# Second norm on ScalarE and turned by TensorE, and fill and drain slots left to the scheduler, in a fused channel-mix and convolution kernel

## The chip, the core and the metric

The kernel runs on one core of a Trainium2 chip. The metric is the device time of one execution in microseconds (us), the median of the runs shown. The engines are TensorE (PE in the profile, with PEld for its weight loads), VectorE (DVE), ScalarE (ACT), GpSimd (POOL) and SyncE (SP), which here only issues DMAs.

## The reference

The input x has 4 images of 128 channels and 128 x 128 positions, in float32. Two layers follow one another. Cut to what matters:

```python
# layer 0, on t = positions x channels (channels are the last axis)
t = ln(gn(x), g0, b0)
y1 = ln(t, g1, b1)
t = t + (sigmoid(y1) * y1) @ W_out.T
y2 = ln(t, g2, b2)                       # the "second norm" of the change
wht = y2 @ W_whiten.T
k = square(relu(wht @ W_key.T))          # 512 hidden channels
t = t + sigmoid(wht @ W_recep.T) * (k @ W_value.T)
x = x + 2 * t                            # two passes, with H and W exchanged, give the same t
# layer 1
out = conv3x3(gn(x)) + bias              # expert 0's weights, 128 -> 128 channels
x = x + out * se[:, :, None, None]       # se: sigmoid of a small MLP on the image's means
```

Here `gn` is a group norm over whole images in groups of four channels, and `ln` a norm over the channels of one position. So the second layer of an image can start only when the first layer of the whole image is done.

## The kernel before

An image is cut into 32 chunks of 512 positions. Two chunks are a pair, called g (0 to 63), with halves h = 0 and 1. A *slot* s is one pass through the list of operations in ORDER; an entry such as `pk01:2` stands for operation pk with half 0 and index 1 on pair g = s - 2. So each slot works on several pairs at once, at different depths, and the list sets the order of instructions on every engine. All slots stand in `tc.manual_schedule()`: there the instructions go to the engines as written. What stands outside it (the set-up, and the convolution of the last image after the slots) is ordered by the scheduler.

For one half the operations are these. `u` (ScalarE) applies the group norm, `Tu` (TensorE, four 128 x 128 transposes) brings positions onto partitions, `bn0` (VectorE) takes the statistics per position, `nb0` (GpSimd, small rows L377 to L388 with a power L382) makes the factors, `t` (ScalarE) scales, and `g` and `b` (GpSimd) apply gain and shift. `bn1`, `nb1`, `z1` (ScalarE), `Tz1`, `silu`, `att`, `T` are the first inner norm and the attention-like part. `tt` turns t back. `bn2` and `nb2` give the factors of the second norm.

The second norm itself: its mean is taken out by weights whose mean over channels is removed at set-up (`mean_of`). Its factor 1/std lies on the partitions, one number a position, but is needed along the free axis. So `Tr` (L429) turns the factors into rt, `rc` (L433) copies it into rrow, `W` (L437) stores it to DRAM, `R` (L442) reads it back spread over all partitions, and `cp` (L446, VectorE) multiplies the turned t by it into y2. Then come `pk` (L450, four matmuls a half into 512 hidden channels), `re` (L454, relu on ScalarE), `sq` (L459, square on ScalarE), `pr` and `th` for the gate, `kv` (L476, four accumulating matmuls), `S` (L486, adds 2t to x), `q` (L492), `x` (L496, GpSimd) and `bx` (L502, statistics for the convolution's group norm).

The convolution of the image before runs in the same slots, from slot 20 on: it is a Winograd form F(4,3) along one axis, with six products c0 to c5 a block of 16 rows (three matmuls each, L514 to L516) and the rest on VectorE. Of its operations half belong to even slots and half to odd ones (EVEN and ODD). The convolution of the last image, 8 blocks, follows after the slots.

PSUM holds eight banks: two each for the tags h (pk, pr), tr (z1t, att, rt, tt) and ut, one for kv and one for conv.

Of the kernel before, what the change touches and what calls it, by code (L numbers as in the profile page):

```python
# [19 lines left out]
LN_EPS = 1e-5  # L20

LAG = 4


ORDER = """
    u1:0 Tu1:0 u0:0 x11:3 Tz10:1 Tu0:0 bn01:0 bn00:0 z11:1 bx1:3 v1:1 pr0:2 Tz11:1 q2:1
    silu0:1 p2:1 re00:2 sq00:2 y2:1 ca:1 att0:1 silu1:1 c0:1 pk01:2 nb0:0 d8:1 kv00:2 T0:1
    y0:1 th0:2 t1:0 bn20:1 v3:1 tt1:2 g1:0 re01:2 in0:0 c1:1 cp1:2 e1:1 att1:1 pk02:2 c3:1
    T1:1 bn21:1 pk10:2 c5:1 b1:0 y3:1 re02:2 S1:2 t0:0 nb2:1 e3:1 pk03:2 v2:1 g0:0 b0:0
    re10:2 c2:1 in1:0 a:1 pk12:2 sq01:2 sq10:2 Tr:1 v0a:1 sq02:2 re03:2 sq03:2 re12:2 b:1  # L30
    kv01:2 kv02:2 rc:1 pk13:2 re13:2 v4:1 pk11:2 kv03:2 sq12:2 c4:0 bn11:0 v5a:0 tt0:1
    bn10:0 v0b:1 pr1:2 q0:2 c:0 d:0 re11:2 sq11:2 S0:1 sq13:2 kv10:2 v5b:0 kv11:2 th1:2
    kv12:2 kv13:2 nb1:0 W:1 y1:0 R0:1 z10:0 q:0 cp0:1 pk00:1 R1:1 x10:2 p:0 bx0:2 q1:2
"""

SQUARES = ("AAAA", "AAAA")

ON_GPSIMD = set()
ODD = {"v5a", "v5b", "c4", "c", "d", "y1", "y2", "ca", "d8", "c0", "y0", "c5", "y3"}
# [7 lines left out]
def conv_preact_kernel(  # L47
# [57 lines left out]
    wk = ctx.enter_context(tc.tile_pool(name="wk", bufs=2))  # L105
    small = ctx.enter_context(tc.tile_pool(name="small", bufs=4))
    stat = ctx.enter_context(tc.tile_pool(name="stat", bufs=2))
    dram = ctx.enter_context(tc.tile_pool(name="dram", bufs=2, space=bass.MemoryType.DRAM))
    ps = ctx.enter_context(tc.tile_pool(name="ps", bufs=2, space=bass.MemoryType.PSUM))

    def bank(tag, name, bufs=2):
        return ps.tile([P, CH], F32, tag=tag, name=name, bufs=bufs)
# [3 lines left out]
    def load_block(g):  # L116
        b, k = g // NBLK, g % NBLK
        blocks[g] = xp.tile([P, BLK], F32, tag="x", name=f"x_{b}_{k}")
        nc.sync.dma_start(
            blocks[g],  # L120
            x[b, :, k * BLK_ROWS : (k + 1) * BLK_ROWS, :].rearrange("c h w -> c (h w)"),
        )
# [20 lines left out]

    nhalf = const.tile([P, N], F32, tag="nhalf", name="nhalf")
    nc.gpsimd.memset(nhalf, -0.5)
    mean_of = const.tile([P, P], F32, tag="mean_of", name="mean_of")
    nc.gpsimd.memset(mean_of, 1.0 / C)

    def load_const(name, src, shape):
        t = const.tile(shape, F32, tag=name, name=name)  # L150
# [22 lines left out]

    wk_s = const.tile([P, HID], F32, tag="wk_s", name="wk_s")
    wr_s = const.tile([P, P], F32, tag="wr_s", name="wr_s")
    kbias = const.tile([P, NH], F32, tag="kbias", name="kbias")
# [2 lines left out]
    def staged(name, n):  # L182
        return wk.tile([P, n], F32, tag="h", name=name, bufs=6)
# [5 lines left out]
    for src, n, dst, bias in ((wkt, HID, wk_s, kbias), (wrt, P, wr_s, rbias)):  # L189
        pw = bank("h", "pw")  # L190
        nc.tensor.matmul(pw[:, :n], ww, src, start=True, stop=True)
        raw, raw2 = staged("raw", n), staged("raw2", HID)
        nc.vector.tensor_copy(raw, pw[:, :n])
        nc.vector.tensor_scalar(raw2[:, :n], raw, g2, None, ALU.mult)
        pc = bank("h", "pc")
        nc.tensor.matmul(pc[:, :n], mean_of, raw2[:, :n], start=True, stop=True)
        nc.vector.tensor_tensor(dst, raw2[:, :n], pc[:, :n], ALU.subtract)
        pb = bank("h", "pb")
        for j in range(n // P):
            nc.tensor.matmul(pb[:, j : j + 1], raw[:, ts(j, P)], b2, start=True, stop=True)  # L200
        nc.vector.tensor_copy(bias, pb[:, : n // P])
# [31 lines left out]
    def input_norm(b):  # L233
        _, mg, rs = yield from group_norm(st0.pop(b), "0")
        nb = col("nb0")
        nc.vector.scalar_tensor_tensor(nb, mg, -1.0, rs, ALU.mult, ALU.mult)
        gn0[b] = rs, nb

    def conv_setup(b):
# [27 lines left out]
        nc.vector.tensor_scalar(dg, ident, se, None, ALU.mult)  # L267
        yield
        pg = bank("h", "pg")
        nc.tensor.matmul(pg[:, :P], mean_of, dg, start=True, stop=True)  # L270
        yield
        row = wk.tile([P, P], F32, tag="u", name="row")
        nc.scalar.mul(row, pg[:, :P], float(C))
        yield
        nc.vector.scalar_tensor_tensor(
            cw, cw, rs, row.rearrange("p (o c) -> p o c", o=1).to_broadcast([P, 9, P]),
# [10 lines left out]
            uw[i] = wg.tile([P, 3, P], F32, tag="uw", name=f"uw{i}", bufs=9)  # L287
            u[i] = uw[i].rearrange("p b c -> p (b c)")

        w6 = wk.tile([P, 3 * P], F32, tag="z", name="w6", bufs=2)  # L290
        nc.scalar.mul(w6, w1, 1.0 / 6)
        tmp = wk.tile([P, 3 * P], F32, tag="u", name="tmp")
        nc.vector.tensor_tensor(tmp, w0, w2, ALU.add)
# [3 lines left out]
        nc.vector.scalar_tensor_tensor(u[1], tmp, -1.0 / 6, w6, ALU.mult, ALU.subtract)  # L297
        nc.vector.scalar_tensor_tensor(u[2], tmp, -1.0 / 6, w6, ALU.mult, ALU.add)
        yield
        w4 = wk.tile([P, 3 * P], F32, tag="z", name="w4", bufs=2)  # L300
        nc.scalar.mul(w4, w0, 0.25)
        nc.scalar.mul(w6, w6, 0.5)
        nc.vector.tensor_tensor(tmp, w4, w2, ALU.add)
# [17 lines left out]
    def flat(t):  # L321
        return t.rearrange("p s c -> p (s c)")
# [23 lines left out]
    def sub_tile(tag, name, bufs):  # L346
        return wk.tile([P, SUB, C], F32, tag=tag, name=name, bufs=bufs)
# [19 lines left out]
    def norm_terms(k, g):  # L367

        st = S.pop(("st", k, g))

        def term(name):
            return small.tile([P, N], F32, tag=f"{name}{k}", name=name, bufs=2)

        gp, rs, nb, sm = nc.gpsimd, term("rs"), term("nb"), term("sm")
        gp.tensor_tensor(rs, st[:, :, 1], st[:, :, 4], ALU.subtract)  # L377
        gp.tensor_tensor(rs, rs, rs, ALU.mult)
        gp.tensor_scalar(rs, rs, C / 4, C * LN_EPS, ALU.mult, ALU.add)
        gp.tensor_tensor(sm, st[:, :, 2], st[:, :, 5], ALU.add)  # L380
        gp.tensor_tensor(rs, rs, sm, ALU.add)
        gp.tensor_tensor(rs, rs, nhalf, ALU.pow)  # L382
        S["norm", k, g] = rs, nb
        if k == 2:
            return
        gp.tensor_tensor(sm, st[:, :, 1], st[:, :, 4], ALU.add)
        gp.tensor_tensor(sm, sm, nhalf, ALU.mult)
        gp.tensor_tensor(nb, sm, rs, ALU.mult)  # L388

    def first_norm(g, h):  # L390
        if ("t", g) not in S:
# [9 lines left out]
        nc.gpsimd.tensor_tensor(t, t, over(b0), ALU.add)  # L401

    def norm(k, g, h):
        S[f"z{k}", g, h] = z = sub_tile("z", "z", 2)
        scaled(z, S["t", g][:, h], S["norm", k, g], h)

    def norm_turned(k, g, h):
# [13 lines left out]
        t = flat(S["t", g][:, h])  # L421
        nc.vector.tensor_tensor(t, S.pop(("att", g, h)), t, ALU.add)

    def turn_std(g):
        rs, _ = S.pop(("norm", 2, g))
        S["rt", g] = rt = bank("tr", "rt")
        nc.tensor.transpose(rt[:N, :P], rs, ident)  # L429

    def copy_std(g):
        S["rrow", g] = row = small.tile([N, P], F32, tag="rrow", name="rrow", bufs=1)
        nc.vector.tensor_copy(row, S.pop(("rt", g))[:N, :P])  # L433

    def store_std(g):
        S["rd", g] = rd = dram.tile([N, P], F32, tag="rd", name="rd")
        nc.sync.dma_start(rd, S.pop(("rrow", g)))  # L437

    def spread_std(g, h):
        S["R", g, h] = r = wk.tile([P, CH], F32, tag="R", name="R", bufs=3)  # L440
        src = S["rd", g][h * SUB : (h + 1) * SUB, :]
        nc.sync.dma_start(r, src.rearrange("(o s) c -> o (s c)", o=1).to_broadcast([P, CH]))  # L442

    def key_input(g, h):
        S["y2", g, h] = y = wk.tile([P, CH], F32, tag="y2", name="y2")
        nc.vector.tensor_tensor(y, flat(S["tt", g, h]), S.pop(("R", g, h)), ALU.mult)  # L446

    def key(g, h, j):
        S["pk", g, h, j] = pk = bank("h", "pk")
# [34 lines left out]
    def add_t(g, h):  # L484
        xs = chunk_of(g, h)
        nc.vector.scalar_tensor_tensor(  # L486
            xs, flat(S["tt", g, h]), 2.0, xs, ALU.mult, ALU.add
        )

    def gated(g, h):  # L490
# [140 lines left out]
    def layer0_op(op, g):  # L631
# [12 lines left out]
            "silu": lambda: silu(g, *d),  # L644
            "att": lambda: attend(g, *d),
            "T": lambda: attended(g, *d),
            "Tr": lambda: turn_std(g),
            "rc": lambda: copy_std(g),
            "W": lambda: store_std(g),
            "R": lambda: spread_std(g, *d),  # L650
            "cp": lambda: key_input(g, *d),
            "pk": lambda: key(g, *d),
            "re": lambda: key_relu(g, *d),
# [32 lines left out]
    for _ in input_norm(0):  # L686
        pass

    with tc.manual_schedule():
        loaded = NBLK  # L690
        for s in range(slots):
            chains = []
            b = s // NP
            if s % NP == NP - 2 and b + 1 < B:
                chains.append(input_norm(b + 1))
            if s % NP == done and 0 < b:
                chains.append(conv_setup(b - 1))
            if s % 2 and s + 1 >= NP and loaded < B * NBLK:
                load_block(loaded)
                loaded += 1  # L700
            for g in reads.get(s, ())[:1]:
                fetch_stats(g)
            for n, (op, k) in enumerate(order):
                g = s - k
                if op in EVEN or op in ODD:
                    c = g - NP - LAG
                    if 0 <= c < (B - 1) * NP and (c % 2 == 1) == (op in ODD):
                        conv_op(op, c // 2)
                elif op in ("in0", "in1"):
                    h = int(op[2])  # L710
                    for i in reads.get(s, ())[:1]:
                        in_stats(i, h, S["in", i][:, ts(h, CH)])
                elif 0 <= g < B * NP:
                    layer0_op(op, g)
                if n % 5 == 4:
                    for chain in chains:
                        next(chain, None)
            for chain in chains:
                for _ in chain:
                    pass  # L720
            for i in reads.get(s, ())[1:]:
                fetch_stats(i)
                for h in range(PAIR):
                    in_stats(i, h, S["in", i][:, ts(h, CH)])


    for k in range((B - 1) * NBLK, B * NBLK):
# [47 lines left out]
```

## Time and profile before

| what | value |
|---|---|
| median of 3 runs (1998.43 to 2006.08) | 2001.2 us |
| the profiled execution, its own time | 2001.2 us |
| its span | 1999.4 us |
| TensorE, VectorE, ScalarE, GpSimd busy | 92%, 67%, 65%, 58% of the span |
| DMA | 130.72 MB, 65 GB/s over the span |

Busy time is a share of the span; a span begins with the first recorded instruction and ends with the last. A row of a group of instructions gives line, engine, operation, tiles, count, busy time, the mean of one in ns, and then the idle time of that engine just before these instructions, with what ended it. TensorE lists one float32 matmul as two instructions, so 128 x 512 matmuls that follow one another take 0.86 us each.

### The profile page before, as it was taken

What the parts mean: (1) busy time and instruction counts of PE and PEld (TensorE: products, weight loads), DVE (VectorE), ACT (ScalarE), POOL (GpSimd) and SP (SyncE); (2) the same over time, 40 slices, a digit from 0 to 9 for tenths busy, and PEclk for the clock granted to TensorE, in tenths of its full rate; (3) what the DMA queues carried; (4) which work ended last, traced back from release to release, by engine and by line L of the source; (5) the groups of instructions that cost most, each with busy time, mean ns of one, the idle gap of its engine ahead of it and who ended that gap; (6) DMA issues with size and microseconds to landing.
All of it is one profiled execution on the core that took longest, in us unless ns stands there. A gap on an engine that the chain in (4) does not pass through costs nothing.

```text
span 1999.4 us, 21672 instructions
## 1 busy us (share of the span) xinstructions
PE 1835.4 (92%) x6154; PEld 937.8 (47%) x6154; DVE 1338.9 (67%) x3276; ACT 1297.7 (65%) x2526; POOL 1151.2 (58%) x1939
## 2 busy tenths in 40 slices
PE   2388888888899999999999999999999999998898
PEld 1244444444455555555455455554454555543343
DVE  5355555555677777687677777766766667664897
ACT  0488787888767676777677777676676777752100
POOL 0577667666666666666566667666566676640000
PEclk9899999999999999999999999999999999998999
DMA  5111111111111222122122222111011111110112
GB/s 196 42 43 43 54 50 57 41 66 65 62 57 61 95 85 85 53 96 76 43 75 85 95 74 86 64 64 55 32 64 64 56 62 64 43 42 33 42 63 84
DMA packets 38567, 130.72 MB, mean 65 GB/s; under 512 B 5408, under 2 KB 7088, under 8 KB 30256
## 3 DMA queue, kind: packets, MB, share of 16 engines
q1 hardware_dynamic: 36160, 128.47, 18.1%
q10 hardware_dynamic: 2288, 0.87, 0.2%
q8 instruction: 49, 0.80, 0.2%
q14 instruction: 70, 0.57, 0.1%
HBM read 95.50 MB, written 33.82 MB: 65 GB/s over the span
## 4 chain that ended last, share of the span: by engine, by line
PE 69%; POOL 12%; DVE 7%; ACT 6%; issue 3%; DMA 2%; ACTq 0%; POOLq 0%; DVEq 0%
PE kv L476 18%; PE pk L450 15%; PE m L514 8%; PE m L515 7%; PE m L516 7%; POOL rs L382 5%; PE pr L467 4%; PE att L418 3%; DVE st L365 3%; ACT t L341 2%; PE ut L334 2%; PE tt L334 2%; PE z1t L334 2%; POOL t L401 1%; ACT z L341 1%
## 5 line engine op out<-in xcount | busy, mean ns | idle before, releaser
L450 PE MATMUL pk<-y,wk_s 128*128 128x512 f32 x1024 | 507.6, 601 | 32.1 <-ACT h L454 23.6
L476 PE MATMUL kv<-h,wv 128*128 128x512 f32 x1024 | 484.8, 596 | 1.4 <-DVE r L492 1.4
L454 ACT ACTIVATE h<-pk,kbias 128x512 f32<-128x512 f32 x512 | 350.8, 689 | 174.5 <-PE pk L450 173.1
L382 POOL TENSOR_TENSOR rs<-rs,nhalf 128x8 f32<-128x8 f32 x192 | 317.4, 1653 | 15.1
L459 ACT ACTIVATE h<-h 128x512 f32<-128x512 f32 x512 | 302.4, 635 | 6.1
L476 PEld LDWEIGHTS kv<-h,wv 128*128 128x128 f32 x1024 | 190.3, 191 | 231.6 <-issue 195.2
L450 PEld LDWEIGHTS pk<-y,wk_s 128*128 128x128 f32 x1024 | 181.2, 190 | 246.1 <-issue 135.9
L341 ACT ACTIVATE t<-ut,nb,rs 128x128 f32<-128x128 f32 x512 | 192.6, 465 | 157.0 <-POOL nb L388 157.0
L496 POOL TENSOR_TENSOR x<-x,r 128x512 f32<-128x512 f32 x128 | 163.1, 1275 | 172.1 <-DVE r L492 172.1
L365 DVE BATCH_NORM_STATS2 st<-t 128x6 f32<-128x128 f32 x1024 | 221.3, 276 | 51.0 <-POOL t L401 47.5
L341 ACT ACTIVATE z<-t,nb,rs 128x128 f32<-128x128 f32 x512 | 209.7, 481 | 52.4 <-POOL nb L388 52.4
L397 POOL TENSOR_TENSOR t<-t,g 128x512 f32<-128x512 f32 x128 | 163.6, 1278 | 101.4 <-ACT t L341 101.4
L514 PE MATMUL m<-v,uw 128*128 128x512 f32 x384 | 202.2, 608 | 15.5 <-ACT e L584 5.9
L377 POOL TENSOR_TENSOR rs<-st 128x8 f32<-128x8 f32 x192 | 56.9, 297 | 258.3 <-DVE st L365 247.2
L515 PE MATMUL m<-v,uw 128*128 128x508 f32 x384 | 197.2, 596 | 0.0
L516 PE MATMUL m<-v,uw 128*128 128x508 f32 x384 | 196.0, 592 | 0.0
L401 POOL TENSOR_TENSOR t<-t,b 128x512 f32<-128x512 f32 x128 | 163.5, 1277 | 10.0
L467 PE MATMUL pr<-y,wr_s 128*128 128x512 f32 x256 | 132.0, 597 | 8.0 <-ACT h L454 8.0
L418 PE MATMUL att<-wo,y 128*128 128x128 f32 x1024 | 137.5, 277 | 0.9 <-ACT y L412 0.7
L365 DVE BATCH_NORM_STATS2 st<-ut 128x6 f32<-128x128 f32 x512 | 111.0, 282 | 37.5 <-PE ut L334 37.5
L492 DVE SCALAR_TENSOR_TENSOR r<-r,kv 128x512 f32<-128x512 f32 x128 | 86.7, 678 | 70.4 <-PE kv L476 65.7
L418 PEld LDWEIGHTS att<-wo,y 128*128 128x128 f32 x1024 | 126.0, 192 | 13.9 <-issue 6.6
(124 smaller groups left out, 2398.3 us busy)
## 6 DMA issues: line engine op xcount, KB each, us to landing
x<-in_x SPq DMA_DIRECT2D x32, 1024.0 KB
R<-rd SPq DMA_DIRECT2D x128, 256.0 KB
out<-x SPq DMA_DIRECT2D x32, 1024.0 KB
xs<-in_x SPq DMA_DIRECT2D x48, 512.0 KB
cw<-in_conv_w SPq DMA_DIRECT2D x4, 576.0 KB
rd<-rrow SPq DMA_DIRECT2D x64, 4.0 KB
wv<-in_w_value_t ACTq DMA_DIRECT2D x1, 256.0 KB
wkt<-in_w_key_t ACTq DMA_DIRECT2D x1, 256.0 KB
```

The source lines that it names most:

```text
L341: nc.scalar.activation(dst[:, s, :], src[:, s, :], AF.Identity, bias=nb[:, i : i + 1], scale=rs[:, i : i + 1],)
L365: nc.vector.bn_stats(st[:, h * SUB + s, :], src[:, s, :])
L382: gp.tensor_tensor(rs, rs, nhalf, ALU.pow)
L418: nc.tensor.matmul(att[:, ts(s, P)], y[:, ts(s, P)], wo, start=True, stop=True)
L450: nc.tensor.matmul(pk, wk_s[:, ts(j, P)], S["y2", g, h], start=True, stop=True)
L454: nc.scalar.activation(k, S["pk", g, h, j], AF.Relu, bias=kbias[:, j : j + 1])
L459: nc.scalar.activation(k, k, AF.Square)
L467: nc.tensor.matmul(pr, wr_s, S["y2", g, h], start=True, stop=True)
L476: nc.tensor.matmul(S["kv", g, h], wv[:, j, :], S.pop(("h", g, h, j)), start=(j == 0), stop=(j == NH - 1))
L514: nc.tensor.matmul(pc, u[:, 1], v, start=True, stop=False)
L515: nc.tensor.matmul(pc[:, :, 1:W], u[:, 0], v[:, :, 0 : W - 1], start=False, stop=False)
L516: nc.tensor.matmul(pc[:, :, 0 : W - 1], u[:, 2], v[:, :, 1:W], start=False, stop=True)
```

## The change

The factors of the second norm are made in full (`nb2` now also gives the shift). ScalarE scales t into z with channels on the free axis (`z2`), TensorE turns it (`Tz2`, four transposes a half, in a tr bank), and ScalarE copies it out of PSUM as y2 (`cp`). The way of the factor over DRAM is gone (`Tr`, `rc`, `W`, `R`), and so is the removal of the mean from the weights. z gets three buffers. Of the four squares of a half the first goes to GpSimd. The list ORDER is a new one, in which nb2 stands a slot later (`nb2:2`) and the key part two or three slots behind (`pk` at 2 and 3, `kv:3`). The body of the loop over slots becomes a function; slots 0 to 2 and those from 64 on stand outside `manual_schedule`.

```diff
+FILL = 3
 ORDER = """
-    u1:0 Tu1:0 u0:0 x11:3 Tz10:1 Tu0:0 bn01:0 bn00:0 z11:1 bx1:3 v1:1 pr0:2 Tz11:1 q2:1
-    silu0:1 p2:1 re00:2 sq00:2 y2:1 ca:1 att0:1 silu1:1 c0:1 pk01:2 nb0:0 d8:1 kv00:2 T0:1
-    y0:1 th0:2 t1:0 bn20:1 v3:1 tt1:2 g1:0 re01:2 in0:0 c1:1 cp1:2 e1:1 att1:1 pk02:2 c3:1
-    T1:1 bn21:1 pk10:2 c5:1 b1:0 y3:1 re02:2 S1:2 t0:0 nb2:1 e3:1 pk03:2 v2:1 g0:0 b0:0
-    re10:2 c2:1 in1:0 a:1 pk12:2 sq01:2 sq10:2 Tr:1 v0a:1 sq02:2 re03:2 sq03:2 re12:2 b:1
-    kv01:2 kv02:2 rc:1 pk13:2 re13:2 v4:1 pk11:2 kv03:2 sq12:2 c4:0 bn11:0 v5a:0 tt0:1
-    bn10:0 v0b:1 pr1:2 q0:2 c:0 d:0 re11:2 sq11:2 S0:1 sq13:2 kv10:2 v5b:0 kv11:2 th1:2
-    kv12:2 kv13:2 nb1:0 W:1 y1:0 R0:1 z10:0 q:0 cp0:1 pk00:1 R1:1 x10:2 p:0 bx0:2 q1:2
+    u1:0 Tu1:0 Tz21:3 u0:0 e1:1 bn01:0 Tu0:0 re02:3 tt0:2 bn00:0 c0:1 cp1:3 sq01:3 c2:1 S0:2
+    q2:1 a:1 re00:3 y0:1 Tz11:1 pk10:3 z10:1 silu1:1 pk13:3 nb0:0 Tz10:1 re10:3 c5:1 re13:3
+    y3:1 sq00:3 att1:1 pr0:3 p2:1 silu0:1 nb2:2 sq03:3 v0b:1 kv00:3 kv01:3 sq02:3 in1:0 b:1
+    t1:0 att0:1 g1:0 v3:1 v4:1 v5a:0 th0:3 kv02:3 t0:0 in0:0 z20:2 b1:0 g0:0 pk12:3 pr1:3
+    re12:3 bn11:0 T1:1 c3:1 sq12:3 T0:1 kv03:3 q0:3 pk11:3 e3:1 th1:3 sq13:3 v5b:0 Tz20:2
+    b0:0 cp0:2 bn10:0 tt1:2 c4:0 re11:3 bn21:1 sq10:3 c:0 y2:0 kv10:3 x10:3 d:0 sq11:3 y1:0
+    z21:2 pk03:2 S1:2 kv11:3 ca:0 q:0 pk01:2 p:0 kv12:3 bx0:3 kv13:3 nb1:0 v1:0 q1:3 x11:3
+    bn20:1 c1:0 bx1:3 z11:0 re01:2 re03:2 pk00:2 v2:0 pk02:2 v0a:0 d8:0
 """
-SQUARES = ("AAAA", "AAAA")
+SQUARES = ("PAAA", "PAAA")
...
-        raw, raw2 = staged("raw", n), staged("raw2", HID)
+        raw = staged("raw", n)
         nc.vector.tensor_copy(raw, pw[:, :n])
-        nc.vector.tensor_scalar(raw2[:, :n], raw, g2, None, ALU.mult)
-        pc = bank("h", "pc")
-        nc.tensor.matmul(pc[:, :n], mean_of, raw2[:, :n], start=True, stop=True)
-        nc.vector.tensor_tensor(dst, raw2[:, :n], pc[:, :n], ALU.subtract)
+        nc.vector.tensor_scalar(dst, raw, g2, None, ALU.mult)
...
-        S["norm", k, g] = rs, nb
-        if k == 2:
-            return
         gp.tensor_tensor(sm, st[:, :, 1], st[:, :, 4], ALU.add)
         gp.tensor_tensor(sm, sm, nhalf, ALU.mult)
         gp.tensor_tensor(nb, sm, rs, ALU.mult)
+        S["norm", k, g] = rs, nb
...
     def norm(k, g, h):
-        S[f"z{k}", g, h] = z = sub_tile("z", "z", 2)
+        S[f"z{k}", g, h] = z = sub_tile("z", "z", 3)
         scaled(z, S["t", g][:, h], S["norm", k, g], h)
...
-    def turn_std(g):
-        rs, _ = S.pop(("norm", 2, g))
-        S["rt", g] = rt = bank("tr", "rt")
-        nc.tensor.transpose(rt[:N, :P], rs, ident)
-
-    def copy_std(g):
-        S["rrow", g] = row = small.tile([N, P], F32, tag="rrow", name="rrow", bufs=1)
-        nc.vector.tensor_copy(row, S.pop(("rt", g))[:N, :P])
-
-    def store_std(g):
-        S["rd", g] = rd = dram.tile([N, P], F32, tag="rd", name="rd")
-        nc.sync.dma_start(rd, S.pop(("rrow", g)))
-
-    def spread_std(g, h):
-        S["R", g, h] = r = wk.tile([P, CH], F32, tag="R", name="R", bufs=3)
-        src = S["rd", g][h * SUB : (h + 1) * SUB, :]
-        nc.sync.dma_start(r, src.rearrange("(o s) c -> o (s c)", o=1).to_broadcast([P, CH]))
-
     def key_input(g, h):
         S["y2", g, h] = y = wk.tile([P, CH], F32, tag="y2", name="y2")
-        nc.vector.tensor_tensor(y, flat(S["tt", g, h]), S.pop(("R", g, h)), ALU.mult)
+        nc.scalar.copy(y, flat(S.pop(("z2t", g, h))))
...
+    def slot(s):
+        ...
+    for s in range(FILL):
+        slot(s)
     with tc.manual_schedule():
-        loaded = NBLK
-        for s in range(slots):
-            ...
+        for s in range(FILL, B * NP):
+            slot(s)
+    for s in range(B * NP, slots):
+        slot(s)
```

The row of ones that spreads the convolution's gain (`mean_of`, scaled back by C) becomes a plain matrix of ones.

More of the change, by code (lines that the diff above doesn't have):

```diff
@@ L107, in conv_preact_kernel @@
     stat = ctx.enter_context(tc.tile_pool(name="stat", bufs=2))
-    dram = ctx.enter_context(tc.tile_pool(name="dram", bufs=2, space=bass.MemoryType.DRAM))
     ps = ctx.enter_context(tc.tile_pool(name="ps", bufs=2, space=bass.MemoryType.PSUM))
@@ L145, in conv_preact_kernel @@
     nc.gpsimd.memset(nhalf, -0.5)
-    mean_of = const.tile([P, P], F32, tag="mean_of", name="mean_of")
-    nc.gpsimd.memset(mean_of, 1.0 / C)
+    ones = const.tile([P, P], F32, tag="ones", name="ones")
+    nc.gpsimd.memset(ones, 1.0)
     def load_const(name, src, shape):
@@ L269, in conv_setup @@
         pg = bank("h", "pg")
-        nc.tensor.matmul(pg[:, :P], mean_of, dg, start=True, stop=True)
+        nc.tensor.matmul(pg[:, :P], ones, dg, start=True, stop=True)
         yield
         row = wk.tile([P, P], F32, tag="u", name="row")
-        nc.scalar.mul(row, pg[:, :P], float(C))
+        nc.scalar.copy(row, pg[:, :P])
         yield
@@ L288, in form @@
             u[i] = uw[i].rearrange("p b c -> p (b c)")
-        w6 = wk.tile([P, 3 * P], F32, tag="z", name="w6", bufs=2)
+        w6 = wk.tile([P, 3 * P], F32, tag="z", name="w6", bufs=3)
         nc.scalar.mul(w6, w1, 1.0 / 6)
@@ L299, in conv_setup @@
         yield
-        w4 = wk.tile([P, 3 * P], F32, tag="z", name="w4", bufs=2)
+        w4 = wk.tile([P, 3 * P], F32, tag="z", name="w4", bufs=3)
         nc.scalar.mul(w4, w0, 0.25)
@@ L486, in add_t @@
         nc.vector.scalar_tensor_tensor(
-            xs, flat(S["tt", g, h]), 2.0, xs, ALU.mult, ALU.add
+            xs, flat(S.pop(("tt", g, h))), 2.0, xs, ALU.mult, ALU.add
         )
@@ L646, in layer0_op @@
             "T": lambda: attended(g, *d),
[L647 to L650, printed above, removed]
             "cp": lambda: key_input(g, *d),
@@ L687, in conv_preact_kernel @@
         pass
-    with tc.manual_schedule():
-        loaded = NBLK
-        for s in range(slots):
[L692 to L724, printed above, removed]
@@ new lines, in slot @@
+    def slot(s):
+        chains = []
+        b = s // NP
+        if s % NP == NP - 2 and b + 1 < B:
+            chains.append(input_norm(b + 1))
+        if s % NP == done and 0 < b:
+            chains.append(conv_setup(b - 1))
+        if s % 2 and s + 1 >= NP and len(blocks) < B * NBLK:
+            load_block(len(blocks))
+        for g in reads.get(s, ())[:1]:
+            fetch_stats(g)
+        for n, (op, k) in enumerate(order):
+            g = s - k
+            if op in EVEN or op in ODD:
+                c = g - NP - LAG
+                if 0 <= c < (B - 1) * NP and (c % 2 == 1) == (op in ODD):
+                    conv_op(op, c // 2)
+            elif op in ("in0", "in1"):
+                h = int(op[2])
+                for i in reads.get(s, ())[:1]:
+                    in_stats(i, h, S["in", i][:, ts(h, CH)])
+            elif 0 <= g < B * NP:
+                layer0_op(op, g)
+            if n % 5 == 4:
+                for chain in chains:
+                    next(chain, None)
+        for chain in chains:
+            for _ in chain:
+                pass
+        for i in reads.get(s, ())[1:]:
+            fetch_stats(i)
+            for h in range(PAIR):
+                in_stats(i, h, S["in", i][:, ts(h, CH)])
```

## Prediction

> **What bounds the kernel now.** I read the page's busy rows first, then the 40 slices, then stretches of one slot, then the chain and the timeline. (A slot is one pass of ORDER, 1024 positions. The first image, slots 0 to 19, has no convolution beside it; slots 20 to 63 have.)
>
> ```profile
> PE 1835.4 (92%) x6154; PEld 937.8 (47%) x6154; DVE 1338.9 (67%) x3276; ACT 1297.7 (65%) x2526; POOL 1151.2 (58%) x1939
> PE   2388888888899999999999999999999999998898
> POOL 0577667666666666666566667666566676640000
> ```
>
> TensorE is nearly full from slice 11 on and at 8 before. The busy time of single slots, first two of the first image and then two with convolution (columns: stretch, length, then PE, PEld, DVE, ACT, POOL, clock, DMA share, GB/s):
>
> ```profile
> 129.21:152.74 23.53, 20.81 (x79) 10.84 (x78) 13.06 (x38) 19.30 (x39) 16.61 (x31) 1.00 0.14 46
> 152.74:176.27 23.53, 20.80 (x79) 10.84 (x78) 13.07 (x38) 19.28 (x39) 16.60 (x31) 1.00 0.14 46
> ...
> 681.10:707.98 26.88, 26.88 (x94) 13.90 (x94) 21.07 (x52) 18.87 (x38) 16.72 (x29) 1.00 0.14 50
> 707.98:737.08 29.10, 28.90 (x99) 14.89 (x98) 19.69 (x49) 21.34 (x42) 19.94 (x32) 1.00 0.28 100
> ```
>
> So there are two regimes. With convolution a pair of slots takes 55.98 us, of which TensorE works 55.78: it alone sets the pace. In the first image a slot takes 23.53 us and no engine fills it: a round of waits does. The chain of waits shows which (start, length, what):
>
> ```profile
> 144.54 0.91 PE att L418 x8
> ...
> 145.54 0.70 DVE t L422
> ...
> 147.81 1.27 POOL t L401
> ...
> 150.42 1.65 POOL rs L382
> 152.08 0.04 issue
> 152.12 0.27 PE rt L429
> 152.40 1.72 PE kv L476 x4
> ```
>
> TensorE, in order, stands before the turn of the second norm's factors (rt) until GpSimd has made them. Edges, from the issue times of L437 and of the u rows: slot 2 starts at 89.3; slot 20 at about 521 (18 slots, 24.0 each); slot 64 at about 1772 (44 slots, 28.43 each, with two of 34.3 where an image begins); then 227.4 to the end. The span is 1999.4, its own time 2001.2, which is the median: I add 1.8 to a span.
>
> **The Trainium skill.** "TensorE: Matmul & The Clock Gate", PE-mode transpose, says that a transpose is a matmul against an identity whose result lands in PSUM and must be copied out: the new path has just these two steps. It gives about 275 ns for one; the trace shows 273 as the duration, but four issue in 0.44 us, and I use 0.11. "GPSIMD Engine Reference", Engine selection, has two-input elementwise work about twice as slow as on VectorE; here 1278 ns against 687. "SBUF — State Buffer", Who interferes with whom: a DVE instruction with two SBUF inputs holds up a GpSimd one that reads SBUF. The trace agrees: a power took 2.08 us beside such VectorE work, 1.64 without it. So GpSimd's sums below are lower bounds once the convolution runs.
>
> **The change, part by part, per slot.**
> - TensorE: 8 transposes of z in (8 x 0.11 = 0.87), the turn of rt out (0.11 of issue): +0.77. Under convolution it is on the path.
> - ScalarE: 8 scalings of z (1.64 for four, so 3.27) and two copies out of PSUM (585 ns from the e copy L586: 1.17) in; two squares out (1.25): +3.2. First-image slots go from 19.3 to 22.5: below 23.5, so no bound by itself.
> - VectorE: two multiplies y (684 ns) and the rrow copy (276) out: -1.64. Worth nothing, TensorE's time covers VectorE in both regimes.
> - GpSimd: three small rows for the second norm (0.27 each with its gap: 0.8) and two squares (taken as 1.28, the nearest row of that size) in: +3.4.
> - SP: the store and two spreads of 256 KB out. Waits on R were 10.2 us in all, most beside a full TensorE: nothing. L623 and L119 then pass no waiting DMA on SP's queue; their tiles are loaded ahead already.
> - Set-up: the matmul and subtraction of the mean go, hidden behind the input statistics (VectorE busy without a gap from 30 to 39.8): nothing. The two statistics of the first xs that the scheduler puts ahead of the aggregation cost up to 1.3.
> - z with three buffers: a bound of 0 to a microsecond per slot of gain; taken as nothing, since no wait on z's release is in the list of waits.
> - The tr banks serve two more tiles in place of one rt, still two banks: their cost lies between nothing and the 0.7 of one wait for the copy y per half. Taken as nothing, the copies stand early in ScalarE's order.
>
> **The order.** The second norm moves a slot later (nb2:2, key part :3), so rt's round is gone. But the new order has its own, on GpSimd: nb0, square, nb2, g1 b1 g0 b0, square, x10, nb1; then ScalarE in order z11, re01, re03, u1, u0; then Tu0, the statistics bn00, and nb0 of the next slot. Priced from the timeline of a first-image slot of before:
>
> ```profile
> 159.20 0.20 POOL L388 TENSOR_TENSOR nb<-sm,rs 128x8 f32<-128x8 f32 x1
> ...
> 164.60 0.21 POOL L377 TENSOR_TENSOR rs<-st 128x8 f32<-128x8 f32 x1 [1.03 <-DVE st L365]
> ...
> 168.18 0.20 POOL L388 TENSOR_TENSOR nb<-sm,rs 128x8 f32<-128x8 f32 x1
> ...
> 170.00 1.27 POOL L397 TENSOR_TENSOR t<-t,g 128x512 f32<-128x512 f32 x1 [1.62 <-ACT t L341]
> 171.35 1.26 POOL L401 TENSOR_TENSOR t<-t,b 128x512 f32<-128x512 f32 x1
> ```
>
> A norm's nine rows take 164.60 to 168.38, 3.8; a large row follows the last by 1.33 (from 170.00 to 171.35, and 1.22 after). From the end of nb (159.40) through z, u, turn and statistics to the next nb0 (164.60) is 5.2; two relus in between add 1.3. Round: 3 x 3.8 + 7 x 1.33 + 5.2 + 1.3 = **27.2 us**, where the old one took 23.5. All of x11 (1.3) lies in the 6.5 outside. In the old order the powers of nb2 stood among g and b, with no square, and only z10 stood between nb1 and u.
>
> **Sum.**
> - Fill: slots 0 to 2 are packed by the scheduler (it lays u of two slots at once), but the pipeline is a slot deeper. GpSimd's rows there: seven to eight norms and twelve large rows from 47.8 on, 8 x 3.8 + 12 x 1.33 = 46, so slot 3 starts near 94, where slot 2 did at 89.3: **+5** (between -5 and +20, the last if the scheduler kept the written order and slot 3 came at 113).
> - First image: 17 slots x 27.2 = 462, and 7 for what 18 slots took beyond 18 x 23.53: 469 against 432: **+37**.
> - With convolution: TensorE 27.9 + 0.77 = 28.7, above the round of 27.2: 44 x 0.77 = **+34**. It is not free of risk: x11 waits for q1 after kv13, late in TensorE's order, and VectorE has bx1, d8 and two statistics between it and nb0.
> - Drain: a slot deeper leaves 15 us more TensorE work behind slot 64 (50 for 34.5); the scheduler may fill part of the 20 or so that before loses from 1823 to 1860 waiting for the last statistics at a cold clock. I take 10 of it: **+5** (-5 to +15).
>
> Together +81: span 2080, time **2082 us**.
>
> **Rivals.**
> - *Slower still (0.15).* The GpSimd round, with VectorE holding its port, passes TensorE with convolution too: a power at 2.08 and a few small rows at 0.6 add 3 us, round 30.2. Then 44 x (30.2 - 28.7) = 66 more, 2148. For it: the round has only 1.5 us to spare; against: VectorE loses 1.64 per slot, and mean powers are 1.65.
> - *The round does not bind (0.12).* If z11 or the relus do not stand as I read them, the first image goes at ScalarE's 22.5 to 23.5: 17 x 23 = 391 + 7, so -71: 2011.
> - *Faster (0.06).* TensorE's wait on rt is the only thing that held the first image, and without it a slot falls to TensorE's own 20.81 - 0.27 + 0.87 = 21.4: 17 x 21.4 = 364, 98 less than 462: 1984. It decides from 21.8 us per slot (1991 is 91 below 2082; 27.2 - 91/17). For it: the chain names rt as the one stall of that stage; against: ScalarE's rows alone are 22.5.
> - *The scheduler changes nothing (0.04).* Fill +20, drain +15: 2107.
>
> **Numbers.** The main case has 0.63, own range 2060 to 2105. About 0.5% (10 us, 1991 to 2011) is what a measurement of this kernel can tell from no change. Faster 0.06; within it 0.06, half of the case without the round; slower 0.88. The range from 2008 to 2125 leaves out the faster case, part of the unbound one and the far part of the first rival, some 0.2 together.
>
> **What would show it.** Right: first-image slots near 27 us with POOL near 20 busy and the chain running through nb, z, u, bn; slots with convolution 28.7 with TensorE full; PE busy +49 in all. Wrong: first-image slots at 23 or below; TensorE idle more than 1 us per slot under convolution, waiting for u or kv's square; a drain shorter than 215.

## The result, and the profile after

The changed kernel takes 2067.7 us (median of 4 runs, 2067.3 to 2074.5) against 2002.0 for the kernel before on the same chip: a ratio of 1.0335, 95% interval 1.0306 to 1.0365. The span of its profiled execution is 2065.5 us, 66.1 over the 1999.4 of before.

From the page of the changed kernel, the busy times and three of the rows in 40 slices:

```profile
PE 1898.8 (92%) x6598; PEld 993.9 (48%) x6598; DVE 1230.4 (60%) x3082; ACT 1489.8 (72%) x3038; POOL 1324.6 (64%) x2259
...
PE   2588888888899999999999999999999999989998
...
ACT  1588888888877887787787887778787887864100
POOL 1667777777767776677667776677677777761000
```

TensorE has 63 us more to do than before, in 66 us more time, so its share stays at 92%. ScalarE gained 192 us of work, GpSimd 173, and VectorE lost 108.5. The first quarter still shows TensorE at 8.

Busy time of single slots of the changed kernel, the same two regimes as before (columns: stretch, length, then PE, PEld, DVE, ACT, POOL, clock, DMA share, GB/s):

```profile
202.08:228.36 26.28, 22.36 (x85) 11.70 (x84) 11.24 (x35) 22.20 (x48) 19.15 (x35) 1.00 0.07 21
228.36:254.63 26.27, 22.35 (x85) 11.69 (x84) 12.49 (x37) 22.18 (x47) 19.15 (x35) 1.00 0.13 41
...
722.21:750.71 28.50, 28.50 (x103) 15.18 (x102) 16.24 (x46) 22.73 (x47) 21.50 (x36) 1.00 0.24 93
750.71:779.50 28.79, 28.70 (x103) 15.27 (x102) 20.71 (x49) 23.59 (x50) 20.39 (x34) 1.00 0.06 18
```

In the first image a slot takes 26.3 us and no engine fills it; with convolution TensorE fills nearly all of 28.5 to 29. The start of each slot is the time of its u row on ScalarE. (Slot 4 is the first that both kernels start in the same way; the scheduler moves the u of slot 3 far ahead in the changed kernel.)

| stretch | before | after | difference | the prediction in these terms |
|---|---|---|---|---|
| start to slot 4 | 137.5 | 123.2 | -14.3 | -16 |
| slots 4 to 19 (first image) | 386.7 (24.2 each) | 425.2 (26.6 each) | +38.5 | +55 |
| slots 20 to 62 (with convolution) | 1219.3 (28.36 each) | 1253.4 (29.15 each) | +34.1 | +33 |
| slot 63 to the end | 255.9 | 263.7 | +7.8 | +9 |

The prediction's own lines start a slot earlier (its fill ends where slot 3 starts); the last column is the same sum cut at slot 4: 94 + 27.6 against 137.5; 16 x 27.6 against 386.7; 43 x 0.77; and the rest of +81.

TensorE's work with convolution, in slots 20 to 62 before and then after (columns as above):

```profile
524.20:1743.52 1219.32, 1199.74 (x4093) 618.20 (x4094) 872.73 (x2138) 869.28 (x1692) 794.18 (x1294) 1.00 0.19 69
548.43:1801.80 1253.37, 1235.34 (x4405) 656.54 (x4404) 800.93 (x2016) 1000.01 (x2036) 911.29 (x1510) 1.00 0.13 49
```

It has 0.83 us more to do a slot and is idle for 0.42 us of a slot, where it was idle for 0.46 before. So these slots grew with its work.

How the first image goes round shows in the timeline of one slot, GpSimd first, then ScalarE:

```profile
205.96 0.21 POOL L373 TENSOR_TENSOR rs<-st 128x8 f32<-128x8 f32 x1 [3.99 <-DVE st L361]
...
209.70 1.04 POOL L435 TENSOR_TENSOR h<-h 128x512 f32<-128x512 f32 x1
210.69 0.21 POOL L373 TENSOR_TENSOR rs<-st 128x8 f32<-128x8 f32 x1
...
225.43 0.20 POOL L381 TENSOR_TENSOR nb<-sm,rs 128x8 f32<-128x8 f32 x1
226.98 1.27 POOL L470 TENSOR_TENSOR x<-x,r 128x512 f32<-128x512 f32 x1 [1.35 <-DVE r L466]
```

```profile
225.66 1.65 ACT L337 ACTIVATE z<-t,nb,rs 128x128 f32<-128x128 f32 x4 [2.99 <-POOL nb L381]
227.22 1.24 ACT L428 ACTIVATE h<-pk,kbias 128x512 f32<-128x512 f32 x2
228.36 1.51 ACT L348 ACTIVATE u<-x,nb,rs 128x512 f32<-128x512 f32 x2
```

GpSimd works from 205.96 to 225.63 without a gap: 19.7 us from nb0 to the end of nb1. ScalarE has stood idle for 2.99 us when nb1 comes, then does z11, the two relus and u, and GpSimd's next nb0 starts one period later, 6.6 us after nb1. 19.7 + 6.6 = 26.3. The list of waits of the changed kernel says the same in totals (who waits, for whom, us, times, longest):

```profile
DVE st L361 <- POOL t L395: 360.5, 66, 15.2
POOL rs L373 <- DVE st L361: 257.6, 69, 8.0
ACT z L337 <- POOL nb L381: 186.6, 83, 6.4
```

Before, ScalarE's z waited 52.4 us for nb in all.

### The profile page after: what moved, and what is told of

It reads as the page before. It is cut to its first block, busy times and chain, and to the rows that moved or that the text cites. A ratio compares the mean times of both kernels' runs of the same rounds, so it can differ in the third digit from the quotient of the medians.

```text
span 2065.5 us, 22717 instructions
## 1 busy us (share of the span) xinstructions
PE 1898.8 (92%) x6598; PEld 993.9 (48%) x6598; DVE 1230.4 (60%) x3082; ACT 1489.8 (72%) x3038; POOL 1324.6 (64%) x2259
## 4 chain that ended last, share of the span: by engine, by line
PE 33%; POOL 12%; ACT 2%; DVE 2%; issue 1%; POOLq 0%; DVEq 0%; ACTq 0%
PE pk L424 8%; PE kv L450 6%; PE m L488 5%; PE m L489 5%; PE m L490 5%; POOL rs L378 3%; POOL t L395 2%; POOL t L391 2%; PE pr L441 1%; ACT z L337 1%; POOL h L435 1%; POOL x L470 1%; PE att L412 1%; PE ut L330 1%; PE z1t L330 1%
## 5 line engine op out<-in xcount | busy, mean ns | idle before, releaser
L424 PE MATMUL pk<-y,wk_s 128*128 128x512 f32 x1024 | 515.9, 606 | 46.0 <-ACT h L428 40.0
L337 ACT ACTIVATE z<-t,nb,rs 128x128 f32<-128x128 f32 x1024 | 421.3, 488 | 186.8 <-POOL nb L381 186.6
L450 PE MATMUL kv<-h,wv 128*128 128x512 f32 x1024 | 510.1, 601 | 26.9 <-POOL h L435 18.3
L428 ACT ACTIVATE h<-pk,kbias 128x512 f32<-128x512 f32 x512 | 341.3, 682 | 59.9 <-PE pk L424 53.2
L450 PEld LDWEIGHTS kv<-h,wv 128*128 128x128 f32 x1024 | 184.3, 191 | 236.8 <-issue 166.7
L470 POOL TENSOR_TENSOR x<-x,r 128x512 f32<-128x512 f32 x128 | 175.3, 1369 | 155.8 <-DVE r L466 155.7
L433 ACT ACTIVATE h<-h 128x512 f32<-128x512 f32 x384 | 234.6, 629 | 4.0
L488 PE MATMUL m<-v,uw 128*128 128x512 f32 x384 | 197.0, 595 | 2.4 <-ACT e L558 0.8
L412 PEld LDWEIGHTS att<-wo,y 128*128 128x128 f32 x1024 | 133.6, 195 | 50.9 <-issue 26.2
L435 POOL TENSOR_TENSOR h<-h 128x512 f32<-128x512 f32 x128 | 134.2, 1048 | 17.9 <-ACT h L428 17.9
```

Of the source, the lines that this page charges most:

```text
L337: nc.scalar.activation(dst[:, s, :], src[:, s, :], AF.Identity, bias=nb[:, i : i + 1], scale=rs[:, i : i + 1],)
L412: nc.tensor.matmul(att[:, ts(s, P)], y[:, ts(s, P)], wo, start=True, stop=True)
L424: nc.tensor.matmul(pk, wk_s[:, ts(j, P)], S["y2", g, h], start=True, stop=True)
L428: nc.scalar.activation(k, S["pk", g, h, j], AF.Relu, bias=kbias[:, j : j + 1])
L433: nc.scalar.activation(k, k, AF.Square)
L450: nc.tensor.matmul(S["kv", g, h], wv[:, j, :], S.pop(("h", g, h, j)), start=(j == 0), stop=(j == NH - 1))
```

## The experiments

Each kernel was timed beside the kernel before, whose median was then 1999.6 to 1999.9 us. Lengths of stretches and slots are of one profiled execution each. An undisturbed slot is one of the usual length of its stage; a few are longer, and are called disturbed.

**1. All squares back on ScalarE.**

```diff
-SQUARES = ("PAAA", "PAAA")
+SQUARES = ("AAAA", "AAAA")
```

> The changed kernel with all squares back on ScalarE; the order stays. Theory A (the GpSimd round nb0, square, nb2, g b g b, square, x10, nb1, then z11, re, re, u, Tu, bn00 sets the first image): two squares of 0.99 us leave the round, so a first-image slot falls from 26.3 to 24.3, ScalarE rises from 22.2 to 23.5 and stays below it; slots with convolution keep 29.1 (TensorE). 17 x 2 = 34 us less, 2033 us. Rival B (ScalarE, 22.2 of work a slot in order, is what holds the first image): slots grow by the 1.25 of two squares, 2067 + 21 = 2088 us or more.

Measured 2064.8 us (ratio to before 1.0321, interval 1.0304 to 1.0339), which can't be told apart from the changed kernel. But the two stages moved, in opposite directions: slots 4 to 19 took 405.9 instead of 425.2 (-19), slots 20 to 62 took 1268.6 instead of 1253.4 (+15, 0.35 a slot). The timeline of GpSimd in a first-image slot of this run:

```profile
201.86 0.21 POOL L373 TENSOR_TENSOR rs<-st 128x8 f32<-128x8 f32 x1 [2.38 <-DVE st L361]
...
219.54 0.20 POOL L381 TENSOR_TENSOR nb<-sm,rs 128x8 f32<-128x8 f32 x1
```

The way from nb0 to nb1 is 17.9 us where it was 19.7, and undisturbed slots are 24.5 to 24.8 where they were 26.3. So the round is what holds the first image, and ScalarE's greater work there is not. The gain is short of the expected 34 us because an undisturbed slot gained 1.6 us and not 2, and the disturbed ones (25.8, 27.4) gave less or nothing. What had not been expected is the loss with convolution. The list of TensorE's waits in slots 20 to 62 of this run shows where it lies:

```profile
PE kv L450 <- ACT h L433: 33.2, 26, 1.3
```

TensorE stands before a kv matmul until ScalarE, in its order, has squared its input: 26 times and 33.2 us in all, where it was 2 times and 4.1 us in the changed kernel. TensorE's idle time rose from 0.42 to 0.93 us a slot.

**2. The squares by image.** Is that loss separate from the gain?

```diff
-        if SQUARES[h][j] == "A":
+        if SQUARES[h][j] == "A" or g < NP + 1:
```

> The changed kernel with the first square of each half on ScalarE for pairs 0 to 16 and on GpSimd after. The run with all squares on ScalarE had a first image 19 us shorter and 0.35 us more per slot with convolution. If these two are separate effects, this one keeps the first and not the second: 2068 - 19 = 2049 us. Rival (the second came from what the first left behind, as a different phase of the pipeline): 2060 us or more.

Measured 2046.0 us (ratio to before 1.0229, interval 1.0213 to 1.0244, where the changed kernel has 1.0335). Slots 4 to 19 took 403.8, slots 20 to 62 took 1250.0: the gain of one and no loss of the other. The waits for ScalarE's square are back at 2 times and 4.1 us. They are separate effects: handing squares to GpSimd cost about 21 us in the first image and saved 15 to 19 with convolution.

**3. The transposes of z2 twice.**

```diff
-        S[f"z{k}t", g, h] = turned(S.pop((f"z{k}", g, h)), "tr", f"z{k}t")
+        z = S.pop((f"z{k}", g, h))
+        S[f"z{k}t", g, h] = zt = turned(z, "tr", f"z{k}t")
+        if k == 2:
+            for s in range(SUB):
+                nc.tensor.transpose(zt[:, s, :], z[:, s, :], ident)
```

> The changed kernel with each transpose of z2 issued twice into the same place (same result): 8 more transposes a slot on TensorE. Theory A (TensorE sets the slots with convolution, the round sets the first image): 0.87 x 44 = 38 us under convolution; in the first image only the four that stand ahead of Tu0 lie in the round, 0.44 x 17 = 7; some 2 in the drain: 2067 + 47 = 2114 us. Rival B (something else, as the GpSimd round or VectorE's order, sets the slots with convolution at 29.1 and TensorE has slack): under 20 us.

Measured 2101.3 us, 34 more. First-image slots went from 26.27 to 26.7, by the 0.44 of the four transposes that lie in the round. With convolution a slot grew by 0.51 (1275.5 for 43), not 0.87. Two of these slots (columns as above):

```profile
730.10:759.50 29.40, 29.40 (x111) 16.15 (x110) 16.48 (x46) 22.80 (x48) 21.53 (x36) 1.00 0.23 91
759.50:788.80 29.30, 29.30 (x111) 16.23 (x110) 20.71 (x48) 23.73 (x50) 20.07 (x34) 1.00 0.06 19
```

TensorE is full in these two. Over all 43 its idle time fell from 0.42 to 0.26 us a slot, which is part of the missing 0.36; the rest doesn't show as idle time. So theory A holds in the main: TensorE sets these slots, with some waits on top that added work hides in part.

**4. All slots as written.** The other half of the change alone, taken away.

```diff
-    for s in range(FILL):
-        slot(s)
     with tc.manual_schedule():
-        for s in range(FILL, B * NP):
+        for s in range(slots):
             slot(s)
-    for s in range(B * NP, slots):
-        slot(s)
```

> The changed kernel with every slot under manual_schedule, the fill and the drain too. Theory A of the prediction: the scheduler's fill is worth 15 to 20 us (slot 3 starts at 97 now, at about 114 here) and its drain about 10: 2092 us. Rival: the scheduler leaves things nearly as they were, within 5 us of 2067.

Measured 2073.1 us: 5 more, not 25. (The two intervals of the ratio, 1.0354 to 1.0385 here and 1.0306 to 1.0365 for the changed kernel, still overlap.) Slot 4 starts at 133.7 instead of 123.2, so packing the fill is worth 10.5 us, half of what was expected. From slot 63 to the end it takes 260.2 us instead of 263.7: in the drain the written order is the shorter one by 3.5 us in these two executions. How large the difference is stays open: the same scheduled drain took 266.2 us in the run of experiment 2. TensorE's rows in the scheduled drain of the changed kernel show where:

```profile
1834.17 3.61 PE L424 MATMUL pk<-y,wk_s 128*128 128x512 f32 x4 [4.03 <-ACT h L428]
...
1859.56 1.13 PE L424 MATMUL pk<-y,wk_s 128*128 128x512 f32 x2 [2.80 <-ACT y L420]
```

Twice TensorE stands before a key matmul while ScalarE has its relu or its copy of z2 late in its order, and after the first of them the four matmuls take 3.61 us instead of 1.88. In the written order neither wait is there, but TensorE waits 8.8 us later on, for VectorE's small steps that set up the last image's convolution (2.7 us in the changed kernel).

**5. The kernel before with scheduled ends.** The same half alone, added: the slot function of the changed kernel, with

```diff
+FILL = 2
```

> The kernel before, with only the other half of the change: slots 0 and 1 and those from 64 on left to the scheduler, second norm and order as before. Theory A (the scheduler's packing is worth as much here as in the changed kernel): slot 2 starts 10 us earlier, the drain loses 10 us less: about 1981 us. Rival (the gain of packing in the changed kernel only pays for its deeper pipeline): 1995 to 2002 us.

Measured 1980.0 us, ratio 0.9902 (0.9885 to 0.9918). Slot 4 starts 4.6 us earlier, and slot 63 to the end takes 243.4 us instead of 255.9. (The profiled execution was the longest of the four, 1985.1 us, so these add up to less than 20.) So this half is worth 20 us on the old second norm and about 5 on the new one; and the rest of the change, between two kernels with scheduled ends, costs 2067.7 - 1980.0 = 88 us. No run takes that rest apart into the new second norm and the new ORDER.

**6. A short round.** The same work, four kinds of entries moved: u and Tu of the next pair a slot ahead (those of pair 0 stand before the first slot), the two relus in front of z11.

```diff
-    u1:0 Tu1:0 Tz21:3 u0:0 e1:1 bn01:0 Tu0:0 re02:3 tt0:2
+    Tz21:3 e1:1 bn01:0 re02:3 tt0:2
...
-    z21:2 pk03:2
+    z21:2 u1:-1 u0:-1 pk03:2
...
-    bx1:3 z11:0 re01:2 re03:2 pk00:2
+    bx1:3 re01:2 re03:2 Tu1:-1 Tu0:-1 z11:0 pk00:2
```

> The changed kernel with the same work and four kinds of entries moved in the order: u and Tu of the next pair go to the end of the slot before (u before z21's successors, Tu behind kv13), and re01, re03 stand ahead of z11. So between nb1 and the next nb0 only x11 and bn00 remain. Theory A (the round sets the first image): a slot there falls from 26.3 towards the sum of ScalarE or TensorE, 22.4, taken as 23; under convolution TensorE stays the bound, 29.1 to 28.9. 16.5 x 3.3 + 44 x 0.2 = 63 us less: 2005 us. Rival (another wait stands right behind: kv10 on GpSimd's square, x11 on q1): first-image slots of 25, about 2045 us.

Measured 2028.1 us, 40 less, ratio 1.0146 (1.0127 to 1.0164). First-image slots fell to 24.6, not to 23: the rival's wait stands right behind. GpSimd and then TensorE in one such slot:

```profile
196.97 1.26 POOL L470 TENSOR_TENSOR x<-x,r 128x512 f32<-128x512 f32 x1 [1.36 <-DVE r L466]
200.63 0.21 POOL L373 TENSOR_TENSOR rs<-st 128x8 f32<-128x8 f32 x1 [2.39 <-DVE st L361]
```

```profile
190.68 1.12 PE L450 MATMUL kv<-h,wv 128*128 128x512 f32 x2 [0.83 <-POOL h L435]
```

VectorE before that nb0:

```profile
198.27 0.69 DVE L476 BATCH_NORM_STATS2 st<-x 128x6 f32<-128x512 f32 x1 [0.60 <-POOL x L470]
198.88 1.67 DVE L361 BATCH_NORM_STATS2 st<-ut 128x6 f32<-128x128 f32 x8
```

TensorE waits for kv10's square; the four kv matmuls end later, so q1 and x11 do, and VectorE, in order, has the statistics of x (bx1) ahead of those of the next ut. Only then comes nb0. With convolution most slots are 28.4 or 28.5, and TensorE is idle for 0.29 us a slot on average.

**7. The short round with the squares by image**, both edits together.

> The short round (2028 us) with the squares of pairs 0 to 16 on ScalarE. In the first image of short_round TensorE stood for kv10 behind GpSimd's square, which put x11 and, on VectorE behind it, the statistics of the next pair late: 24.6 a slot. Theory A (that chain is the second round): with the square on ScalarE a slot comes near ScalarE's sum of 23.4, taken as 23.7: 16 x 0.9 = 14 us less, 2014 us. Rival (another chain stands there, or ScalarE's order now does): 2025 us or more.

Measured 2030.9 us: the rival. The slots are 24.8. kv10 now stands 1.35 us for its square on ScalarE (L433), where it stood 0.83 on GpSimd's: the square is as late in one engine's order as in the other's. The chain of experiment 6 is not shown to be the last one; what would bring these slots to ScalarE's 22.9 stays open.

**8. The kernel before with scheduled ends and a later turn.**

```diff
-    sq10:2 Tr:1 v0a:1
+    sq10:2 v0a:1
...
-    kv01:2 kv02:2 rc:1 pk13:2 re13:2 v4:1
+    kv01:2 kv02:2 Tr:1 pk13:2 re13:2 rc:1 v4:1
```

> The kernel before with scheduled ends (1980 us), and the turn Tr behind kv01 and kv02 and its copy rc behind pk13, so that TensorE has 1.7 us of other work while GpSimd makes the factors. Theory A (TensorE's in-order wait on rt, 1.4 us a slot in the first image, is what holds 23.5 there): 22.2 a slot, 18 x 1.3 = 24 us less, 1956 us. Rival B (the row of factors over DRAM arrives later by as much and the keys wait for it, under convolution too): no gain, or up to 1 us a slot more, 1980 to 2024 us.

Measured 1989.0 us, 9 more than without it: theory A was wrong. TensorE no longer waits for rt, yet first-image slots only went from 23.5 to 23.3. The timeline of TensorE in such a slot shows who is next:

```profile
181.15 0.66 PE L335 MATMUL ut<-ident,u 128*128 128x128 f32 x4 [1.09 <-ACT u L353]
```

In this run ScalarE idles 2.34 us for nb1, then does z10 and u (from 178.75 to 181.81), and TensorE waits for u: GpSimd's round, which the old kernel has too, of 23.3 us. With convolution the slots grew by 0.25; no run shows why.

**9 and 10. The kernel before with scheduled ends and u and Tu a slot ahead**, with the late turn and without it (u and Tu of pair 0 stand before the first slot, as in experiment 6).

```diff
-    u1:0 Tu1:0 u0:0 x11:3 Tz10:1 Tu0:0 bn01:0
+    x11:3 Tz10:1 bn01:0
...
-    kv12:2 kv13:2 nb1:0
+    u1:-1 u0:-1 kv12:2 kv13:2 Tu1:-1 Tu0:-1 nb1:0
```

> The kernel before with scheduled ends and the late turn (1989 us), and u and Tu of the next pair at the end of the slot before. In the late-turn run the first image was held at 23.3 by nb0, g b, nb2, g b, nb1, z10, u, Tu, bn00 on GpSimd, ScalarE, TensorE and VectorE. Theory A (there are two rounds of nearly one length, rt's of 23.5 and GpSimd's of 23.3, and both are cut here): about 21.8 a slot, 17 x 1.5 = 25 us less: 1964 us. Rival (a third wait): 1980 us or more.

> The kernel before with scheduled ends (1980 us) and u and Tu of the next pair at the end of the slot before; the turn where it was. Theory A (two rounds): the round of 23.3 is cut, rt's of 23.5 stays, so the first image stays at 23.5 a slot and the time at 1980 us, within 8. Rival (the GpSimd round alone held the first image and rt's wait only followed it): 22 a slot, about 1955 us.

Measured 1954.7 us with the late turn and **1952.4 without it**, ratio 0.9759 (0.9744 to 0.9773): the shortest times of all, too close to tell apart. Both expectations missed. With the late turn, undisturbed first-image slots are 22.6, not 21.8, and the time is 9 us below the forecast because the slots with convolution gained too. Without it, theory A had 1980 us and 23.5 a slot, and the slots are 22.9, though rt is where it was. The time is near the rival's 1955, but that rival said that rt's wait only follows GpSimd's round. TensorE in one first-image slot of experiment 5, then in one of this run without the late turn:

```profile
290.80 0.27 PE L430 MATMUL rt<-ident,rs 128*8 128x128 f32 x1 [1.43 <-POOL rs L383]
...
300.79 0.60 PE L335 MATMUL ut<-ident,u 128*128 128x128 f32 x4
```

```profile
283.81 0.27 PE L430 MATMUL rt<-ident,rs 128*8 128x128 f32 x1 [1.41 <-POOL rs L383]
...
292.94 1.04 PE L335 MATMUL ut<-ident,u 128*128 128x128 f32 x8
```

The wait for rt is still there. But the edit also moves Tu ahead of pk00 in TensorE's order, so from rt to the next Tu it is now 9.1 us where it was 10.0. The edit meant for GpSimd's round shortens rt's round as well, by about the 0.7 us that a slot lost; so the two can't be told apart by this run, and rt's round may well be what still sets 22.9.

Without the late turn the span is 32 us below that of experiment 5 (28 by the medians). By u times, 6 of these lie before slot 3, 11 in slots 3 to 19 and 17 in slots 20 to 62, and the part from slot 63 on is 3 longer. (u itself stands earlier in its slot here, so the first and the last of these are shifted a little.) Of the 17, 6 lie where an image begins: the two slots there take 60.2 us together, where they took 63.1, and this happens twice.

## Why the prediction was right, and where not

The forecast was 2082 us (2008 to 2125), the result 2067.7, slower as foretold; three of its four terms stand within 3 us of the measurement, two of them by luck.

- **First image, +37 at a slot of 27.2 us: the term that was mis-sized.** The mechanism is as written: nb0 to nb1 on GpSimd, then z11, the relus, u, Tu, bn00. The way outside GpSimd is 6.6 us (6.5 predicted). The way on GpSimd is 19.7 (20.7 predicted): a square of a tile with itself takes 0.99 to the next row, not the 1.33 taken from the gain row, two of them 0.7; and the other large rows follow one another at 1.28 on average. With 26.3 in place of 27.2, and 5 us of disturbed slots in place of 7, the term is 17 us smaller: all of the difference. That the round decides was tested from three sides: 1.8 us of squares taken out of it gave 1.6 a slot (experiment 1), 0.44 put into it gave 0.43 (3), and moving four kinds of entries without any change of work gave 1.6 (6). (The prediction's 7 us for disturbed slots come out as 8 by its own edges, 432 - 18 x 23.53; that is small beside the rest.)
- **With convolution, +34: right,** 34.1 over 43 slots, 0.79 each. TensorE's work grew by 0.83 a slot there (0.77 predicted), and its idle time stayed near 0.4. The slots are 29.15 on average, not 28.7: that figure is TensorE's work (28.73 measured), and the idle time comes on top, as it did before. In all TensorE's busy row grew by 63 us, not by the foretold 49: most of the excess lies in the first image, where a slot shows 22.36 of work for 20.81 before. What stretches the rows there is not shown.
- **Fill and drain, +5 each: the nets are right, their parts are not, and that is luck.** The fill's packing was taken as 19 us and is 10.5; but the new order reaches slot 4 earlier even as written (133.7 against 137.5). In the drain the scheduler was to save 10 of 15 us; it loses some 3.5, and the changed kernel as written costs 4 (260.2 against 255.9) rather than 15. Two errors cancel in each. The cold clock that the prediction names there does show in the kernel before: from 1823.5 to 1864 the granted clock was 0.76 on average, and TensorE worked for 25.4 of these 40.5 us.
- **The z buffers, the tr banks, SP's queue, VectorE at nothing:** no run took these apart. VectorE's saving of 1.6 us a slot shows as busy time (1.7); whether any of it is in the time was not tested.
- **ScalarE "no bound by itself".** Its 22.2 a slot was right (22.5), and in the first image two more squares on it did not hold the round up. Under convolution they cost 0.35 a slot, which the sum of its work (23.6 + 1.25 of 29) did not tell: what counted was when ScalarE came to a square that TensorE stood waiting for.
- **The rival that the round does not bind** and **the faster one** fall with the measured slot of 26.3 and with experiment 1: without the wait on rt the slot did not go to 21.4. (With the 0.11 that the list of parts uses for the turn, in place of 0.27, that figure would be 21.6.) The run with rt moved shows why rt was never alone: the old kernel had GpSimd's round of 23.3 behind rt's 23.5. The prediction named rt as the only round there, from a chain that shows one of two nearly equal ones. This bears on the faster rival alone: the price of the new round did not rest on it. **The slower rival** did not come: with convolution the slots stayed at TensorE's pace. Its slow powers are rare: 4 of the 192 took 2.08 to 2.20 us in the kernel before, and 4 took 1.97 to 3.14 in the changed one. "1.64 without it" also holds for more than was said: in the kernel before, powers beside VectorE work on two SBUF tiles that began after the power had took 1.64 too.

## What to carry to other kernels

Where no engine is full, follow one slot round: sum the in-order work from an operation to its own next turn, engine by engine. Here that sum, and not any engine's busy time, was the slot, and work moved into or out of it counted nearly in full (0.43 for 0.44, 1.6 for 1.8), though the engine looked idle for a quarter of the slot. A chain view shows one such round, so before taking one away, look for the next of nearly the same length, and check whether an edit meant for one round also shortens another. A small move of entries that lets an engine do its next slot's first operations while it waits gave 40 us in the changed kernel and 28 in the old one, where the change cost 38.5 in the first image and 34 with convolution. Between the best orders found on either side (2028.1 and 1952.4 us) the new second norm still stands 76 us behind; no run shows how far either order is from its best.

## What the runs showed of the hardware that was not expected

In the changed kernel a GpSimd multiply of a 128 x 512 float32 tile with itself took 1.04 us, where two different tiles took 1.27 to 1.28. And after TensorE stood still for 4.03 us in the drain, four matmul instructions that took 1.88 us together at a granted clock of 1.00 took 3.61, at a granted clock of 0.52. The same wait in the run of experiment 2 was followed by 3.78 us at 0.50.
